# Node numbering, adjacency pieces and the start of layer 0 in a four-layer graph network

## The chip, the core and the metric

One core of a Trainium2 chip runs the whole network in one launch. The metric is the device time of a run in microseconds. The engines named below are PE (TensorE, with PEld for its weight loads), DVE (VectorE), ACT (ScalarE), POOL (GpSimd) and SP (SyncE, which issues most of the DMAs here).

## What is computed

The input `x` has 16 batches of 1024 nodes with 64 features, float32; `adj` is one 1024 x 1024 int32 adjacency for all batches. Four layers follow each other. Each adds its output to its input and normalizes the rows.

```python
x = layernorm(x + L0(x, adj))   # graph attention: leaky_relu(s1[i] + s2[j]), masked softmax, elu
x = layernorm(x + L1(x, adj))   # softplus features, a masked softmax per feature
x = layernorm(x + L2(x, adj))   # like L0, other weights
x = layernorm(x + L3(x, adj))   # 4 heads of masked softmax(h h^T) h, then one outer such layer
```

In layers 0 to 2 the mask is the adjacency; in layer 3 it is `adj + eye > 0`. Entries of `adj` of zero or below count as no edge.

## The kernel before

**Tiles.** P is 128 and C is 8: the nodes are cut into eight chunks of 128, one node to a partition. Node number `p * 8 + c` lies in partition p, chunk c, so a partition holds eight rows of `x` that are neighbours in memory (`load_x`, L641: 2 KB in memory, but eight runs of 256 bytes in the tile `xg`, where four batches share a chunk). The stores at L1549 and L1554 use the same numbering; there both sides are 2 KB runs.

**The adjacency.** `load_adj` (L806) loads eight tiles `adj`, tile c with the rows `p * 8 + c`, each row whole (4 KB), through four buffers. `adjacency` (L813) makes of one tile: `gr`, its 0/1 form in bfloat16 (DVE, L815); on ACT the sum of what lies below zero, kept in `adj_low` (`below`, L817); eight transposes on PE (L821) of every eighth column into PSUM (`paT`); and one copy of that (L822, DVE for even c, ACT for odd c) into `aT`. `aT[:, k, :]` is the mask that chunk k of the neighbours needs for all 1024 nodes, and every one of the eight tiles gives a strip of 128 columns of it. So no mask of layer 0 can start before all eight tiles are done. `adj_low` is checked at the end of the program (L1919): if it is not zero, a general path is run.

**Layer 0 and layer 2** (`gat_layer`, L900). For every pair of batches a chain prepares the factors: `prep_x` transposes x (`pxT`, L919, and its copy `xT`, L920), `prep_s` makes the scores of the nodes (`ps`, L926), `prep_top` reduces them to a largest one (`l_s`, `top`, and an all-reduce on POOL, L937), `prep_p` makes `p` and `q` on ACT, `prep_G` a matmul `pg` (L960) and its exponential `G_l` (L961, one for each half of the nodes, PSUM for one `pg` at a time), and `prep_v` the values `vals_l` (L967). Then, for each batch and chunk k, `unit(k)` makes a mask product `e` on DVE (L980) from G, q and `aT[:, k, :]`, and `product(k, e)` multiplies it on PE with the values: `y_l` (L992) for each chunk and, in layer 0, `u_l` (L1004) for four chunks at once, which adds up the weights.

**What sets the order.** Within `gat_layer`'s loop over batches t and chunks k (L1156), the order on PE, ACT, DVE and POOL is the order in which the code issues the instructions (`manual_schedule`). `behind` (L792) keeps a product back until `lag` more masks are issued: four in layer 0, two in layer 2. `slots` holds the tasks of the chains and of the ends of earlier batches, by (t, k). What comes ahead of the loop, `first(ahead)` (L1663), is ordered by the scheduler: it loads the adjacency, x 2 and 3, the weights and the other x, then makes the eight pieces, one after the other, with one task of the first pair's chain behind each. DMAs of SP are issued in order, and one that needs a buffer back waits for it with all behind it.

**Layer 3.** `aT` gets the diagonal (L1857). Masks multiply `e` on DVE (L1328) ahead of the product on PE (L1335); scores are made on PE (L1320) and exponentiated on ACT (L1324). Scores and masks of a burst of three or five units are issued before the products of the burst before. For the outer layer the adjacency is also needed the other way round, `aN`: `nodes_adj(c)` (L1237) loads the same rows of `adj` again, `convert` turns them into 0/1 (L1242, reading every eighth element) and adds the diagonal. The eight conversions lie in the bursts of the first batch. `aN` is read by the outer layer's sums (L1432).

Of the kernel before, what the change touches and what calls it, by code (L numbers as in the profile page):

```python
# [582 lines left out]
def fast_path(  # L583
# [49 lines left out]
    def xb(b):  # L633
        return xg[b // GB][:, :, b % GB, :]
# [3 lines left out]
        return xg[b // GB][:, c, b % GB : b % GB + 2, :].rearrange("p b d -> p (b d)")  # L638

    def load_x(b):  # L640
        nc.sync.dma_start(xb(b), x[b].rearrange("(p c) d -> p c d", c=C))  # L641


    nc.scalar.preload_act_table_set("natural_log_exp_and_others")
# [159 lines left out]
    adj_v = adj.rearrange("(p c) n -> c p n", c=C)  # L804

    def load_adj(stage):  # L806
        tiles = []
        for c in range(C):
            tiles.append(stage.tile([P, N], I32, tag="adj", name=f"adj{c}", bufs=4))
            nc.sync.dma_start(tiles[c], adj_v[c])  # L810
        return tiles

    def adjacency(stage, a_sb, c):  # L813
        gr = stage.tile([P, N], BF16, tag="gr", name=f"gr{c}")
        nc.vector.tensor_scalar(gr, a_sb, 0.0, None, ALU.is_gt)  # L815
        below = stage.tile([P, N], BF16, tag="below", name="below", bufs=1)
        nc.scalar.activation(below, a_sb, AF.Relu, scale=-1.0, accum_out=adj_low[:, c : c + 1])  # L817
        gr_v = gr.rearrange("p (q k) -> p k q", k=C)
        pt = ps_t.tile([P, C, P], BF16, tag="t", name="paT")
        for k in range(C):  # L820
            nc.tensor.transpose(pt[:, k, :], gr_v[:, k, :], ident16)  # L821
        (nc.scalar.copy if c % 2 else nc.vector.tensor_copy)(aT[:, :, c * P : (c + 1) * P], pt)  # L822

# [7 lines left out]
    def gat_weights(W, a, name, zero_mean, queue):  # L831
        wd = const.tile([P, D], F32, tag=f"{name}_wd", name=f"{name}_wd")
        w1 = const.tile([P, P], F32, tag=f"{name}_w1", name=f"{name}_w1")
        w4 = const.tile([P, 4], F32, tag=f"{name}_w4", name=f"{name}_w4")
        ind = const.tile([P, 2], F32, tag=f"{name}_ind", name=f"{name}_ind")
        s12 = const.tile([P, B // 2, C, 4], F32, tag=f"{name}_s", name=f"{name}_s")
        sums = const.tile([P, B, C], F32, tag=f"{name}_sums", name=f"{name}_sums")
        checks.append((s12, sums))
        a_sb = const.tile([D, 2], F32, tag=f"{name}_a", name=f"{name}_a")
        queue.dma_start(a_sb, a.rearrange("(t o) u -> o (t u)", o=D))  # L840
        for i in range(2):
            queue.dma_start(wd[i * D : (i + 1) * D, :], W)
        return dict(wd=wd, w1=w1, w4=w4, ind=ind, s12=s12, sums=sums, a=a_sb)
# [56 lines left out]
    def gat_layer(w, name, zero_mean, extra, first, own, ordered):  # L900
# [249 lines left out]
        for (t, k), todo in extra.items():  # L1150
            for task in todo:
                at(t, k, task)
        first(ahead)
        if ordered:
            run.enter_context(tc.manual_schedule(engines=in_order))
        for t in range(B + 1):  # L1156
            for k in range(C):
                catch_up()
                if t < B:
                    unit, product, _ = work[t]  # L1160
                    e = unit(k)
                    behind(lambda product=product, k=k, e=e: product(k, e), LAG if zero_mean else 2 * LAG)
                elif t == B and k == 0:
                    drain()
                if t < B or (t == B and k < own):
                    for task in slots.get((t, k), []):
                        task()
# [68 lines left out]

    def nodes_adj(c):  # L1237
        a_sb = l3.tile([P, N], I32, tag="e", name=f"adj3_{c}", bufs=11)
        nc.sync.dma_start(a_sb, adj_v[c])

        def convert():
            nc.vector.tensor_scalar(  # L1242
                aN[:, c, :].rearrange("p (k q) -> p k q", q=P), a_sb.rearrange("p (q k) -> p k q", k=C),
                0.0, None, ALU.is_gt,
            )
# [168 lines left out]
    def head_out(b):  # L1414
# [129 lines left out]
        def rows():  # L1544
            shift = small.tile([P, C], F32, tag="ln_ve", name="ln_shift")
            nc.vector.tensor_tensor(shift, held["less"], held["rstd"], ALU.mult)
            res = ep.tile([P, C, D], F32, tag="m", name="res", bufs=4)
            scaled(res, held["m"], (held["rstd"], shift), range(C))
            nc.sync.dma_start(out[b].rearrange("(p c) d -> p c d", c=C), res)  # L1549

        def finish():
            res = ep.tile([P, C, D], F32, tag="m", name="res", bufs=4)
            nc.vector.tensor_tensor(res, held["m"], bc_last(held["rstd"], D), ALU.mult)
            nc.sync.dma_start(out[b].rearrange("(p c) d -> p c d", c=C), res)  # L1554
# [103 lines left out]
    with tc.tile_pool(name="ps_g", bufs=1, space=bass.MemoryType.PSUM, reuse_waits="tile") as ps_g, tc.tile_pool(  # L1658
        name="ps_u", bufs=2, space=bass.MemoryType.PSUM, reuse_waits="tile"
    ) as ps_u, tc.tile_pool(name="gat0", bufs=2, reuse_waits="tile") as gp:  # L1660
        later = {}

        def first(ahead):  # L1663
            with tc.tile_pool(name="stage", bufs=2, reuse_waits="tile") as stage:
                tiles = load_adj(stage)
                load_x(2)
                load_x(3)
                later["w2"] = gat_weights(L2_W, L2_a, "l2", True, nc.sync)
                later["tasks", "w2"] = gat_setup(later["w2"], "l2", True)
                later["tasks", "w3"] = layer3_weights(gp)  # L1670
                layer1_weights()
                for b in range(4, B):
                    load_x(b)
# [12 lines left out]
        l1["psum"] = lambda name: ps_g.tile([P, 2, HALF], F32, tag="g", name=name).rearrange(  # L1686
            "p i (c q) -> p (i c) q", q=P
        )
        l1_tasks = [prep_l1(0, q) for q in range(2)]
        extra = {}  # L1690
        for t, k in ((2, "w2"), (4, "w3")):
            for i, n in enumerate((2, 3, 4, 5)):
                extra[t, n] = [lambda k=k, i=i: later["tasks", k][i]()]
        for q, todo in enumerate(l1_tasks):
            t = 7 + 2 * q
            places = (t, 0), (t, 2), (t, 4), (t, 6), (t + 2, 2), (t + 2, 7), (t + 3, 5)
            for place, task in zip(places, todo):
                extra.setdefault(place, []).append(task)
        ending = gat_layer(w_0, "l0", False, extra, first, 5, True)
# [278 lines left out]
```

## Time and profile before

| | |
|---|---|
| median of 3 runs | 2076.14 us (2075.71 to 2076.99) |
| the profiled execution | 2073.99 us, its span 2072.2 us |
| PE busy | 1960.6 us, 95% of the span |
| DVE busy | 1795.4 us, 87% |
| ACT busy | 1294.2 us, 62% |
| POOL busy | 69.3 us, 3% |
| mean granted PE clock | 0.978 of full speed |
| DMA | 18.92 MB in 23657 packets |

Spans, durations and waits in the views are of the one profiled execution, counted in microseconds from the start of its span. A row of a timeline gives the start, the time from the first to the last of the instructions in it, the engine, the line, the operation, the tile written and the tiles read, and in brackets how long the engine had been idle and who ended that. A row of a stage gives the busy time of each engine in it with the number of instructions, then the clock that PE was granted (1.00 is full), the mean busy share of the DMA engines and the GB/s that they moved. A row of one line's instructions gives the shortest, median and longest duration in ns. A row of waits gives the total, the number of times and the longest wait in us.

### The profile page before, as it was taken

Reading aid. Unit: us, or ns where it says so; the run is one execution under the profiler, and the core shown is the slowest. Engines: PE = TensorE matmul, PEld = TensorE weight load, DVE = VectorE, ACT = ScalarE, POOL = GpSimd, SP = SyncE. Lnnn points to the kernel's source line nnn. Section 1 sums busy time; section 2 is a strip of 40 time slices with the busy share of each in tenths; the row PEclk is TensorE's granted clock in tenths of the full one; section 3 lists DMA queues with packets and bytes.
Section 4 is the critical chain, followed back from the end, with each engine's and each line's share of the span. In section 5 each row is a group of like instructions: output and inputs, shape, how many; then the busy total and the mean of one; then the engine's idle time right before and its main releaser. Section 6 shows DMA issues by size and latency. Waiting matters only on the chain.

```text
span 2072.2 us, 26628 instructions
## 1 busy us (share of the span) xinstructions
PE 1960.6 (95%) x10041; PEld 851.5 (41%) x10041; DVE 1795.4 (87%) x3147; ACT 1294.2 (62%) x2250; POOL 69.3 (3%) x77
## 2 busy tenths in 40 slices
PE   7999989998888999999999999999999999999985
PEld 4444357843332344343343434334343343433332
DVE  5899988869998777889898898988989889889996
ACT  5456568666778666666666656655665666665543
POOL 0000000000000000000000000000000000000001
PEclk8999999989999999999999999999999999999997
DMA  6000000000000200000000000000000000000000
GB/s 170 1 1 1 1 1 0 1 1 1 1 1 12 70 1 1 1 1 6 1 6 6 1 6 6 1 6 1 6 3 3 6 1 6 6 1 6 1 6 17
DMA packets 23657, 18.92 MB, mean 9 GB/s; under 512 B 19361, under 2 KB 19426, under 8 KB 23522
## 3 DMA queue, kind: packets, MB, share of 16 engines
q1 hardware_dynamic: 23218, 17.11, 2.9%
q8 instruction: 81, 1.33, 0.3%
q14 instruction: 54, 0.44, 0.1%
q10 hardware_dynamic: 304, 0.03, 0.0%
HBM read 12.95 MB, written 4.19 MB: 8 GB/s over the span
## 4 chain that ended last, share of the span: by engine, by line
PE 46%; DVE 38%; ACT 12%; issue 3%; DMA 0%; POOL 0%; SPq 0%; DVEq 0%; POOLq 0%; ACTq 0%
DVE e L1328 13%; PE y L1335 10%; PE s L1320 8%; DVE e L980 6%; PE y_l L992 6%; ACT e L1324 6%; PE po L1712 4%; DVE e L1440 4%; DVE junk L1432 4%; PE u_l L1004 3%; PE y L1447 2%; PE po L1350 2%; ACT e L1427 2%; PE s L1422 2%; DVE v L1360 2%
## 5 line engine op out<-in xcount | busy, mean ns | idle before, releaser
L1324 ACT ACTIVATE e<-s,shift 128x1024 f32<-128x1024 f32 x512 | 542.8, 1119 | 335.2 <-PE s L1320 334.3
L1328 DVE TENSOR_TENSOR e<-e,aT 128x1024 f32<-128x1024 f32 x512 | 600.6, 1217 | 4.9 <-ACT e L1324 4.8
L1335 PE MATMUL y<-e,vals 128*64 128x512 f32 x2048 | 489.5, 600 | 11.0 <-DVE e L1328 5.9
L1320 PE MATMUL s<-hT 64*128 64x512 f32 x2048 | 497.7, 605 | 1.3 <-ACT e L1324 0.9
L980 DVE SCALAR_TENSOR_TENSOR e<-G_l,q,aT 128x1024 f32<-128x1024 f32 x256 | 315.3, 1274 | 10.3 <-ACT G_l L961 10.2
L1320 PEld LDWEIGHTS s<-hT 64*128 64x128 f32 x2048 | 186.9, 187 | 279.6 <-issue 140.3
L992 PE MATMUL y_l<-e,vals_l 128*64 128x512 f32 x1024 | 254.7, 618 | 24.4 <-DVE e L980 22.6
L1335 PEld LDWEIGHTS y<-e,vals 128*64 128x64 f32 x2048 | 134.9, 136 | 277.7 <-issue 189.3
L1440 DVE TENSOR_TENSOR e<-e,aT 128x1024 f32<-128x1024 f32 x128 | 156.3, 1224 | 8.3 <-ACT e L1427 1.9
L1432 DVE SCALAR_TENSOR_TENSOR junk<-e,aN 128x1024 bf16<-128x1024 f32 x120 | 146.1, 1217 | 0.0
L1427 ACT ACTIVATE e<-s,shift 128x1024 f32<-128x1024 f32 x128 | 142.0, 1115 | 1.2 <-PE s L1422 1.1
L1447 PE MATMUL y<-e,h2v 128*64 128x512 f32 x512 | 131.2, 595 | 1.6 <-DVE e L1440 1.6
L1422 PE MATMUL s<-h2T 64*128 64x512 f32 x512 | 131.7, 596 | 0.0
L992 PEld LDWEIGHTS y_l<-e,vals_l 128*64 128x64 f32 x1024 | 62.6, 138 | 159.4 <-issue 75.9
L1712 PE MATMUL po<-hi,aR 128*128 128x512 f32 x256 | 102.4, 401 | 13.6 <-ACT hi L1648 8.6
L1712 PE MATMUL po<-lo,aR 128*128 128x512 f32 x256 | 100.8, 394 | 0.0
L780 ACT ACTIVATE x<-m,bn_shift,bn_rstd 128x64 f32<-128x64 f32 x256 | 88.5, 431 | 2.4 <-DVE bn_shift L771 2.4
L1263 POOL PARTITION_ALL_REDUCE gtop<-top x48 | 42.7, 890 | 1375.8 <-DVE top L1261 1169.0
L1350 PE MATMUL po<-wb,yT 128*128 128x130 f32 x512 | 74.2, 288 | 10.0 <-ACT e L1324 9.4
L1350 PEld LDWEIGHTS po<-wb,yT 128*128 128x128 f32 x512 | 61.9, 190 | 47.4 <-ACT e L1324 45.8
L1422 PEld LDWEIGHTS s<-h2T 64*128 64x128 f32 x512 | 49.8, 188 | 61.2 <-issue 28.4
L1384 ACT COPY zT<-pzT 128x1024 f32<-128x1024 f32 x32 | 32.8, 1025 | 66.9 <-PE pzT L1383 66.9
(241 smaller groups left out, 2028.6 us busy)
## 6 DMA issues: line engine op xcount, KB each, us to landing
adj<-in_adj_dram SPq DMA_DIRECT2D x16, 512.0 KB, 4.2
x<-in_x_dram SPq DMA_DIRECT2D x16, 256.0 KB, 5.0
out_dram<-res SPq DMA_DIRECT2D x16, 256.0 KB, 2.0
wl<-in_L_gnn_Wh_dram SPq DMA_DIRECT2D x2, 64.0 KB, 3.6
wo<-in_L_gnn_Wo_dram SPq DMA_DIRECT2D x1, 64.0 KB, 3.1
l_wd<-in_L_gnn_W_dram ACTq DMA_DIRECT2D x2, 16.0 KB, 4.1
l_wd<-in_L_gnn_W_dram SPq DMA_DIRECT2D x2, 16.0 KB, 2.2
bo<-in_L_gnn_bo_dram SPq DMA_DIRECT2D x1, 32.0 KB, 3.2
```

What stands on the lines that cost most here:

```text
L980: nc.vector.scalar_tensor_tensor(e, G[b - b % 2][:, b % 2, :], pq[b - b % 2][1][:, k, b % 2 : b % 2 + 1], aT[:, k, :], ALU.max, ALU.mult,)
L992: nc.tensor.matmul(held["y"][h * D : (h + 1) * D, :], vals[b][:, k, :], e[:, h * HALF : (h + 1) * HALF], start=(k == 0), stop=(k == C - 1),)
L1320: nc.tensor.matmul(s[:, i, :], hT[rows, k * P : (k + 1) * P], hT[rows, cols], start=True, stop=True)
L1324: nc.scalar.activation(e, s, AF.Exp, bias=shifts[b, n])
L1328: nc.vector.tensor_tensor(e, e, bc_mid(aT[:, k, h * HALF : (h + 1) * HALF], 2), ALU.mult)
L1335: nc.tensor.matmul(held[h][i * D : (i + 1) * D, :], vals[b][:, k, :], e[:, i, :], start=(k == 0), stop=(k == C - 1),)
L1350: nc.tensor.matmul(o[:, j // 2, j % 2, :], held["y"][:, j * P : (j + 1) * P], wb[:, n, :], start=True, stop=True,)
L1422: nc.tensor.matmul(s[:, i, :], hT[rows, (i + k // CH) % 2, k % CH * P : (k % CH + 1) * P], hT[rows, 0, :], start=True, stop=True,)
L1427: nc.scalar.activation(e, s, AF.Exp, bias=shifts[b])
L1432: nc.vector.scalar_tensor_tensor(junk.rearrange("p c q -> p (c q)").bitcast(BF16), e.rearrange("p i q -> p (i q)"), 1.0, aN[:, k, :], ALU. ...
L1440: nc.vector.tensor_tensor(e, e, aT[:, k, :].rearrange("p (i q) -> p i q", i=2), ALU.mult)
L1712: nc.tensor.matmul(po.rearrange("p q k f -> p (q k f)"), aR[:, k, ic * P : (ic + 1) * P], e[:, k].rearrange("p q k f -> p (q k f)"), start ...
```

## The change

Nodes are numbered `c * 128 + p`: chunk c is the 128 rows from `c * 128`. x and the result are read and written in that order. For layer 0 the adjacency is loaded by columns: piece c holds the columns of chunk c for all rows (1024 runs of 512 bytes), into the ring that the masks use, and `aT[:, c, :]` comes from that piece alone. All eight loads are issued without waiting for a buffer, x 2 and 3 between the fourth and the fifth. The sum on ACT of what lies below zero goes; in layer 3, where the rows are loaded again, DVE takes each row's minimum, and the check is that it is not below zero. The conversion there reads and writes in order. Every copy into `aT` is on ACT. Three pieces are made ahead of the loop, behind the third, the fourth and the sixth task of the chain; the other five come in the loop, each behind one of the first five masks of layer 0. While those come, and in the whole first batch, a product waits for one to three masks instead of four.

```diff
     def load_x(b):
-        nc.sync.dma_start(xb(b), x[b].rearrange("(p c) d -> p c d", c=C))
+        nc.sync.dma_start(xb(b), x[b].rearrange("(c p) d -> p c d", c=C))
...
-    def load_adj(stage):
-        tiles = []
-        for c in range(C):
-            tiles.append(stage.tile([P, N], I32, tag="adj", name=f"adj{c}", bufs=4))
-            nc.sync.dma_start(tiles[c], adj_v[c])
-        return tiles
+    def load_adj(c):
+        t = gp.tile([P, C, P], I32, tag="e", name=f"adj{c}", bufs=10)
+        nc.sync.dma_start(t, adj[:, c * P : (c + 1) * P].rearrange("(k p) q -> p k q", p=P))
+        return t
...
-    def adjacency(stage, a_sb, c):
-        gr = stage.tile([P, N], BF16, tag="gr", name=f"gr{c}")
+    def adjacency(a_sb, c):
+        gr = gp.tile([P, C, P], BF16, tag="gr", name=f"gr{c}", bufs=3)
         nc.vector.tensor_scalar(gr, a_sb, 0.0, None, ALU.is_gt)
-        below = stage.tile([P, N], BF16, tag="below", name="below", bufs=1)
-        nc.scalar.activation(below, a_sb, AF.Relu, scale=-1.0, accum_out=adj_low[:, c : c + 1])
-        gr_v = gr.rearrange("p (q k) -> p k q", k=C)
         pt = ps_t.tile([P, C, P], BF16, tag="t", name="paT")
         for k in range(C):
-            nc.tensor.transpose(pt[:, k, :], gr_v[:, k, :], ident16)
-        (nc.scalar.copy if c % 2 else nc.vector.tensor_copy)(aT[:, :, c * P : (c + 1) * P], pt)
+            nc.tensor.transpose(pt[:, k, :], gr[:, k, :], ident16)
+        nc.scalar.copy(aT[:, c, :], pt.rearrange("p k q -> p (k q)"))
...
-        first(ahead)
+        stream = first(ahead) or []
...
-                    behind(lambda product=product, k=k, e=e: product(k, e), LAG if zero_mean else 2 * LAG)
+                    lag = LAG if zero_mean else 2 * LAG
+                    if stream or (t == 0 and not zero_mean):
+                        lag = 1 + k // 3
+                    behind(lambda product=product, k=k, e=e: product(k, e), lag)
+                    if stream:
+                        stream.pop(0)()
...
     def nodes_adj(c):
         a_sb = l3.tile([P, N], I32, tag="e", name=f"adj3_{c}", bufs=11)
-        nc.sync.dma_start(a_sb, adj_v[c])
+        nc.sync.dma_start(a_sb, adj[c * P : (c + 1) * P, :])
...
-            nc.vector.tensor_scalar(
-                aN[:, c, :].rearrange("p (k q) -> p k q", q=P), a_sb.rearrange("p (q k) -> p k q", k=C),
-                0.0, None, ALU.is_gt,
-            )
+            nc.vector.tensor_scalar(aN[:, c, :], a_sb, 0.0, None, ALU.is_gt)
+            nc.vector.tensor_reduce(adj_low[:, c : c + 1], a_sb, AX.X, ALU.min)
...
-            nc.sync.dma_start(out[b].rearrange("(p c) d -> p c d", c=C), res)
+            nc.sync.dma_start(out[b].rearrange("(c p) d -> p c d", c=C), res)
...
         def first(ahead):
-            with tc.tile_pool(name="stage", bufs=2, reuse_waits="tile") as stage:
-                tiles = load_adj(stage)
...
-                for c in range(C):
-                    adjacency(stage, tiles[c], c)
-                    for task in ahead[c : c + 1]:
-                        task()
-                for task in ahead[C:]:
-                    task()
+            tiles = [load_adj(c) for c in range(CH)]
+            load_x(2)
+            load_x(3)
+            tiles += [load_adj(c) for c in range(CH, C)]
...
+            for i, task in enumerate(ahead):
+                task()
+                if i in (2, 3, 5):
+                    adjacency(tiles[(2, 3, 5).index(i)], (2, 3, 5).index(i))
...
+            return [lambda c=c: adjacency(tiles[c], c) for c in range(3, C)]
...
-    check(adj_low, ALU.is_le, 0.0)
+    check(adj_low, ALU.is_ge, 0.0)
```

More of the change, by code (lines that the diff above doesn't have):

```diff
@@ L803, in fast_path @@
     adj_low = const.tile([P, C], F32, tag="adj_low", name="adj_low")
-    adj_v = adj.rearrange("(p c) n -> c p n", c=C)
-    def load_adj(stage):
-        tiles = []
-        for c in range(C):
-            tiles.append(stage.tile([P, N], I32, tag="adj", name=f"adj{c}", bufs=4))
-            nc.sync.dma_start(tiles[c], adj_v[c])
-        return tiles
-    def adjacency(stage, a_sb, c):
-        gr = stage.tile([P, N], BF16, tag="gr", name=f"gr{c}")
+    def load_adj(c):
[4 more added lines that the diff above has]
+        gr = gp.tile([P, C, P], BF16, tag="gr", name=f"gr{c}", bufs=3)
         nc.vector.tensor_scalar(gr, a_sb, 0.0, None, ALU.is_gt)
-        below = stage.tile([P, N], BF16, tag="below", name="below", bufs=1)
-        nc.scalar.activation(below, a_sb, AF.Relu, scale=-1.0, accum_out=adj_low[:, c : c + 1])
-        gr_v = gr.rearrange("p (q k) -> p k q", k=C)
         pt = ps_t.tile([P, C, P], BF16, tag="t", name="paT")
         for k in range(C):
-            nc.tensor.transpose(pt[:, k, :], gr_v[:, k, :], ident16)
-        (nc.scalar.copy if c % 2 else nc.vector.tensor_copy)(aT[:, :, c * P : (c + 1) * P], pt)
+            nc.tensor.transpose(pt[:, k, :], gr[:, k, :], ident16)
+        nc.scalar.copy(aT[:, c, :], pt.rearrange("p k q -> p (k q)"))
     checks = []
@@ L1553, in finish @@
             nc.vector.tensor_tensor(res, held["m"], bc_last(held["rstd"], D), ALU.mult)
-            nc.sync.dma_start(out[b].rearrange("(p c) d -> p c d", c=C), res)
+            nc.sync.dma_start(out[b].rearrange("(c p) d -> p c d", c=C), res)
         units = [
@@ L1663, in first @@
         def first(ahead):
-            with tc.tile_pool(name="stage", bufs=2, reuse_waits="tile") as stage:
-                tiles = load_adj(stage)
[L1666 to L1673, printed above, removed]
-                for c in range(C):
-                    adjacency(stage, tiles[c], c)
-                    for task in ahead[c : c + 1]:
-                        task()
-                for task in ahead[C:]:
-                    task()
+            tiles = [load_adj(c) for c in range(CH)]
+            load_x(2)
+            load_x(3)
+            tiles += [load_adj(c) for c in range(CH, C)]
+            later["w2"] = gat_weights(L2_W, L2_a, "l2", True, nc.sync)
+            later["tasks", "w2"] = gat_setup(later["w2"], "l2", True)
+            later["tasks", "w3"] = layer3_weights(gp)
+            layer1_weights()
+            for b in range(4, B):
+                load_x(b)
+            for i, task in enumerate(ahead):
+                task()
+                if i in (2, 3, 5):
+                    adjacency(tiles[(2, 3, 5).index(i)], (2, 3, 5).index(i))
             l1["pool"] = l1_pools.enter_context(
```

## The prediction, made before the changed kernel ran

> **What bounds the kernel now.** I read the page's list of groups first (PE is busy 1960.6 of 2072.2 us), then the timeline of the first 75 us, then the busy time by stage in steps of 2 us, and last the waits of PE in layer 3 and the timeline of the end. Comparing the two instruction orders, engine by engine, I find that they differ in three places only: before about 50 us, in eight added vector instructions of layer 3, and in the shape of the DMAs. So the sum has three terms.
>
> The timeline of the start, at the steps that count:
>
> ```profile
> 15.12 0.69 DVE L822 COPY aT<-paT 128x1024 bf16<-128x1024 bf16 x1 [2.10 <-PE paT L821]
> ...
> 21.95 1.07 PE L821 MATMUL paT<-ident,gr 128*128 128x128 bf16 x8 [0.25 <-DVE gr L815]
> ...
> 24.09 1.10 ACT L961 ACTIVATE G_l<-pg,up 128x1024 f32<-128x1024 f32 x1
> ...
> 27.42 1.97 PE L919 MATMUL pxT<-ident,x 128*128 128x128 f32 x8
> ...
> 28.68 2.48 DVE L980 SCALAR_TENSOR_TENSOR e<-G_l,q,aT 128x1024 f32<-128x1024 f32 x2 [2.06 <-ACT G_l L961]
> ...
> 31.18 3.58 PE L926 MATMUL ps<-l_w,xT_l 128*128 128x4 f32 x16 [1.79 <-ACT xT_l L920]
> ...
> 34.68 5.03 PE L992 MATMUL y_l<-e,vals_l 128*64 128x512 f32 x16
> ...
> 50.08 1.94 PE L992 MATMUL y_l<-e,vals_l 128*64 128x512 f32 x8
> ```
>
> All eight pieces are transposed before the first mask (28.68). That mask waits for G, not for the adjacency. From 31.18 PE never rests: batch 2's `ps`, batch 0's products from 34.68, batch 1's from 50.08. A mask that comes early therefore gains only what PE can use. The stages (columns: PE, PEld, DVE, ACT, POOL, clock, DMA, GB/s):
>
> ```profile
> 4.00:6.00 2.00, 0.00 (x0) 0.00 (x0) 0.00 (x0) 0.00 (x0) 0.00 (x0) 1.00 1.04 235
> ...
> 8.00:10.00 2.00, 1.10 (x8) 1.08 (x9) 1.86 (x11) 1.47 (x4) 0.00 (x0) 1.00 1.03 422
> ...
> 14.00:16.00 2.00, 2.00 (x20) 1.63 (x19) 0.88 (x2) 1.97 (x4) 0.00 (x0) 1.00 0.72 256
> ...
> 32.00:34.00 2.00, 2.00 (x11) 2.00 (x11) 0.00 (x0) 0.00 (x0) 0.00 (x0) 0.50 1.18 212
> ...
> 38.00:40.00 2.00, 2.00 (x12) 0.44 (x12) 2.00 (x3) 2.00 (x9) 0.00 (x0) 1.00 1.35 222
> ```
>
> The clock is at half from 17 to 37.5 us, so the small `ps` products cost 3.58 us there against 1.90 at 14.91. DMA moves about 235 GB/s in 256-byte pieces (x) and 422 GB/s in 4 KB rows (adjacency).
>
> **Term 1, the start: about +3.2 us.** I walk the new order with durations from these rows.
>
> *DMA.* A piece is 512 KB in 512-byte runs, 1024 of them. Bounds: 512 KB at 422 GB/s is 1.25 us, at 235 is 2.2; I take 1.8, nearer to x's small pieces. The first landed at 7.15; now 7.6, then 9.4, 11.2, 13; after x2 and x3, the last at about 23. The first mask comes later than most of these, so this costs nothing up to about 3 us a piece. Beyond that every mask waits.
>
> *Up to G.* PE no longer puts a transposed piece between x's: `pxT` 10.1 to 12.1 (8 for 1.97), `ps` and one `pg` to 15.4. DVE makes top by 15.8, and the all-reduce returns 2 us later (top at 35.02, down at 37.77 now). PE does pieces 0 to 2 to 18.4. ACT loses eight `below` (1.06 and 0.19 each, 10 us) but copies every aT: its order has three copies (1.01) before p, so p starts at 19.5, G at 20.0 (24.09 now), `vals` (2.0) at 21.1, the second G at 23.4 (its `pg` is done at 23.2), the first mask at 24.5: 4.2 us early. DVE is spared four aT copies of 0.69.
>
> *After it.* DVE's order is e0, gr3, e1, gr4: 1.21 and 0.69 each. gr3 is done at 26.4, and only then can PE transpose piece 3: it has rested from 18.4 to 21.2 and from 23.2 to 26.5, 6 us, in which the old order did this work. A mask's product is a quarter of sixteen records (3.58 at 42.63 in the chain), so 0.9 at full and 1.76 at half speed. From 26.5 PE's queue runs without a gap: piece 3 1.04, `pxT` of batch 2 2.2, `ps` 3.58 (33.3); y0 1.76, piece 4 1.04, y1 1.76 (37.9, clock full again); pieces 5 and 6 1.41 (0.70 each, the row at 14.37), y2 0.9, piece 7 0.8, y3 0.9, u 1.85, y4 0.9, `pg` 1.06, y5 to y7 2.7, u 1.85, `pg` 1.06, `pxT` 1.03. Batch 1's product starts at 52.4, against 50.08: **+2.3**. Queued behind each gr on DVE are the next mask and, behind gr4, batch 2's l_s; who waits is PE. From there the order is the old one and PE is the bound, so the difference stays.
>
> *The clock.* The trace's full speed at 14 to 17 us follows a stretch in which PE streamed without a pause (10.2 to 13.6). The new order has 128x4 products in it, which nearest rows (30 to 34 us, half speed) do not speed up. Without that stretch the second half of `ps`, two pieces and `pg` are slow, G is at 22.6 and batch 1 at 54.9: +4.8 against this trace. The old order without it would lose 1.9 in the same walk, leaving +2.9. Bounds +0.5 (fast before `ps` of batch 2 by luck of phase, whose 3.58 would be 1.9) and +4.8; I take 3.2.
>
> The Trainium skill ("TensorE: Matmul & The Clock Gate", section "Part 1: The HAM clock gate") says some 3.4 us of sustained PE work give the full clock. The trace disagrees for narrow work: at 32 to 34 us PE is 2.00 of 2.00 busy at 0.50. By the rule alone PE, busy from 26.5, would be fast at 30 to 33 and this term about +1.
>
> **Term 2, layer 3: about +1.0 us.** Each of eight conversions loses its stride and gains a reduction to one minimum.
>
> ```profile
> L1242 DVE TENSOR_SCALAR aN<-adj x8: 1082/1084/1094, 673.7 to 731.8; 128x1024 bf16<-128x1024 int32 x8
> ```
> ```profile
> L815 DVE TENSOR_SCALAR gr<-adj x8: 681/693/694, 7.2 to 23.7; 128x1024 bf16<-128x1024 int32 x8
> ```
> ```profile
> 2051.55 0.81 DVE L1914 TENSOR_REDUCE flags<-ok 128x1 f32<-128x640 f32 x1
> ```
>
> Conversion 1.08 becomes 0.69; a reduction of 1024 is 0.81 x 1024/640 less its fixed part (512 take 0.68), 1.21. That is +0.82 each, 6.5 us of DVE. What hides it is PE, which waits for no mask there:
>
> ```profile
> PE y L1335 <- ACT yT L1341: 1.0, 1, 1.0
> PE s L1320 <- ACT e L1324: 0.9, 1, 0.9
> PE po L1350 <- ACT e L1324: 0.6, 1, 0.6
> ```
>
> DVE idles 12.8 us for PE between 677 and 737 (3.35, 2.92, 1.48, 2.01, 3.02). Of these only 1.48 follows the two conversions at 698 and 703, which add 1.64, so there a little gets through. Bounds 0 and 6.5; I take one conversion and a little, 1.0. A gain is excluded: aN is read first past 760 us. The `below` work that this replaces was in term 1.
>
> **Term 3, the end: about +0.8 us.** The last store now has 1024 pieces of 256 bytes where it had 128 of 2 KB.
>
> ```profile
> 2066.78 0.33 SPq L1554 DMA_DIRECT2D out_dram<-res  x1
> ```
>
> Nothing lies beside it. The issue of x's like-shaped load takes 0.55 at least (+0.2); 256 KB at 235 GB/s is 1.1 us, at 422 is 0.6 (+0.5). Bounds: +0.2, if stores pipeline, and +1.8 (x's loads take 3.5 to land, stores 2.0, and the issue); I take 0.8. The earlier 15 stores have cover. The Trainium skill ("DMA: Bandwidth & Descriptors", "Specifications") names 512 bytes as the least for line rate, with read-modify-write below; no run here shows it for stores. By it this term would lean to its upper bound, and adjacency pieces would take 1.25 us.
>
> **Sum.** +3.2 +1.0 +0.8 = +5.0. The profiled execution took 2073.99 (span 2072.2 and 1.8 around it), so 2079.0 for one like it. The runs' median is 2076.14, 2.15 above it, so **2081.1**.
>
> **Rivals.**
> *A, PE pays (forecast), 0.58:* five transposes move from PE's idle time into its full queue. For it: 34.68 onward is gapless. 2080.3 to 2085.
> *B, it evens out, 0.28:* PE gets the full clock early in its new queue (term 1 +0.5 to 2), layer 3 hides all, the store costs 0.3: +1 to +4, 2077 to 2080. Same mechanism, small.
> *C, faster, 0.06:* the mask's 4.2 us lead reaches PE. It needs y0 right behind e0 at 26, which decides from the point where PE runs `pxT` and `ps` of batch 2 inside the rests at 18.4 and 23.2 and the clock is full by 26. Then at best -4.2 to -5, nothing lost later: 2071.5. Against it: `ps` stands ahead of y0 on PE.
> *D, the pieces land slowly, 0.08:* over 3 us for 512-byte runs at a 4 KB pitch. At 4 us each the last lands near 40, gr5 to gr7 hold the masks, batch 1 starts at about 62: +14 with the other terms, 2088 to 2092. For it: nothing here shows such a load.
>
> The measurement can tell about 0.2% (4.2 us) from no change. Slower is A and D, 0.66; same is B, 0.28; faster is C, 0.06. The range leaves out C, the low edge of B and the worst of D: 2077 to 2086.5; the slower cases' own range is 2080.3 to 2087.
>
> **What would show it.** Right: first mask at 24 to 27 us; PE rests of 2 to 4 us on both sides of the second `pg`; first y_l at 33 to 36 after `ps`; batch 1's y_l at 52 to 55; the reductions at 1.2 us with PE waiting under 2 us for masks in 670 to 745; the last store landing 0.5 to 1.5 us later. Wrong: y_l within 3 us of the first mask (C); gr waiting for a DMA after 15 us (D); a half-speed clock ending before 33 us (B).

## The result, and the profile after

| | before | after |
|---|---|---|
| median of 22 runs each, taken together | 2074.28 us (2071.43 to 2076.99) | 2079.01 us (2076.35 to 2082.81) |
| ratio | | 1.0025 [1.0019, 1.0031] |
| the profiled execution, its span | 2073.99, 2072.2 us | 2082.49, 2080.7 us |

The changed kernel is slower by 4.7 us between the medians, or 3.9 to 6.4 us by the interval. The forecast was 2081.1 us, a difference of +5.0 us to the median of three runs known then; that of 22 old runs lies 1.9 us lower. In the experiments below, one run of e7 took 3997.19 us, far from every other, and is left out. The profiled execution of the changed kernel happens to be one of its longest, so its span overstates the difference (+8.5 us); I split that first.

Matched instruction by instruction, the difference between the two profiles is +5.59 us when batch 1's first `y_l` begins and stays at that value to the end of layer 0. It is about 7.9 us after a stretch of half-speed clock at 338 to 342 us that the old kernel's profile doesn't have, 7.5 us through layer 3, 8.9 us at the last `res`, and 8.5 us at the end. Where such stretches fall differs from profile to profile (further down), so I don't count the part after layer 0 as the change's.

The busy times of the page after say which engine pays:

```profile
PE 1966.3 (95%) x10041; PEld 853.5 (41%) x10041; DVE 1797.7 (86%) x3151; ACT 1289.4 (62%) x2238; POOL 69.7 (3%) x77
```

PE has as many instructions as before (10041), but is busy 5.7 us longer (1960.6 before): the same work, more of it at half clock. A part of the 5.7 us is the stretch at 338 us. (The mean granted clock, 0.983 in this profile and 0.978 before, can't show it, since it counts the first 41.3 us as full; see below.) ACT is only 4.8 us less busy, although 10 us of `below` are gone: four more `aT` copies of about 1 us went to it. The timeline of the start (start, time, engine, line, operation, tile written and read, and in brackets the idle time of the engine and who ended it):

```profile
12.35 1.87 PE L921 MATMUL ps<-l_w,xT_l 128*128 128x4 f32 x8
...
14.15 2.07 PE L955 MATMUL pg<-xT_l,l_w 64*128 64x512 f32 x2
16.16 1.87 PE L921 MATMUL ps<-l_w,xT_l 128*128 128x4 f32 x8
...
19.68 2.07 PE L955 MATMUL pg<-xT_l,l_w 64*128 64x512 f32 x2
21.68 1.04 PE L816 MATMUL paT<-ident,gr 128*128 128x128 bf16 x8
...
23.67 0.31 ACT L943 ACTIVATE p<-l_s,down 128x16 f32<-128x16 f32 x1
...
24.07 1.10 ACT L956 ACTIVATE G_l<-pg,up 128x1024 f32<-128x1024 f32 x1
...
25.23 2.08 PE L955 MATMUL pg<-xT_l,l_w 64*128 64x512 f32 x4 [2.51 <-ACT G_l L956]
...
28.50 1.28 DVE L975 SCALAR_TENSOR_TENSOR e<-G_l,q,aT 128x1024 f32<-128x1024 f32 x1 [9.28 <-ACT G_l L956]
...
30.45 1.04 PE L816 MATMUL paT<-ident,gr 128*128 128x128 bf16 x8 [3.14 <-DVE gr L813]
...
33.49 3.42 PE L921 MATMUL ps<-l_w,xT_l 128*128 128x4 f32 x16
36.84 1.98 PE L987 MATMUL y_l<-e,vals_l 128*64 128x512 f32 x4
...
55.67 1.94 PE L987 MATMUL y_l<-e,vals_l 128*64 128x512 f32 x8
```

and of the old kernel:

```profile
24.41 1.07 PE L821 MATMUL paT<-ident,gr 128*128 128x128 bf16 x8 [1.39 <-DVE gr L815]
...
25.41 2.08 PE L960 MATMUL pg<-xT_l,l_w 64*128 64x512 f32 x4
```

The `pg` of the first half of the nodes stands in two rows here, 64 matrix rows for each batch of the pair (14.15 and 19.68, the first and the second `pg` below); the third row (25.23) is that of the second half, both batches side by side.

Three things are to be seen. First, G starts at 24.07, where it started before (24.09): nothing that ACT was spared has arrived. p, which stands ahead of G on ACT, has its `up` and `down` at 19.2, but ahead of it in ACT's order stands the copy of piece 2, whose transposes stand on PE behind the second `pg` and end at 22.7. Second, PE rests 2.51 us ahead of the next `pg` (25.23) and 3.14 us ahead of piece 3 (30.45): together 5.65, against 1.39 and 1.79 in the old kernel. Third, from the third `pg` to batch 1's `y_l` it is now 30.44 us (25.23 to 55.67), and was 24.67 (25.41 to 50.08). In it PE makes five pieces, 3.76 us, and rests 1.6 us more; these are 5.4 of the 5.8 us. The interval also holds more half clock (25.23 to 41.3, and 25.41 to 37.5 before), so a part of these prices is the clock's; e3 and e4 below take that apart.

The clock is at half throughout: 16 `ps` products take 3.42 us at 33.49, and full speed comes only at 41.3 us (37.5 before, after a stretch of full speed at 14 to 17 that is not here). One stage of 2 us (PE, PEld, DVE, ACT, POOL, clock, DMA, GB/s):

```profile
34.00:36.00 2.00, 2.00 (x11) 2.00 (x11) 0.00 (x0) 0.32 (x1) 0.00 (x0) 1.00 1.36 217
```

The column prints 1.00 there although the products take twice their time: it does so in every stage ahead of the first change of clock that a trace records. At the start the clock is to be read from durations.

The adjacency, by the rows of its eight loads (issue in ns, then the landing):

```profile
L808 SPq DMA_DIRECT2D adj<-in_adj_dram x8: 926/1410/2656, 1.8 to 15.5; - x8
...
DMA to landing us min/median/max: 5.7/7.1/8.0
```

The last is issued at 15.5 and is there by 24, ahead of the first mask; no gr waits for a transfer after 12 us. In the stages with the most traffic (6 to 12 and 16 to 20 us) the core moved 283 to 313 GB/s, and 422 in the old kernel's 4 KB rows.

Layer 3, the rows of the conversion and of the new reduction, and PE's waits from 655 to 770 us (total, times, longest):

```profile
L1244 DVE TENSOR_REDUCE adj_low<-adj x8: 1206/1210/1212, 681.9 to 740.5; 128x1 f32<-128x1024 int32 x8
...
L1243 DVE TENSOR_SCALAR aN<-adj x8: 681/684/686, 681.3 to 739.9; 128x1024 bf16<-128x1024 int32 x8
```
```profile
PE y L1334 <- ACT yT L1340: 1.0, 1, 1.0
PE s L1319 <- ACT e L1323: 0.9, 1, 0.9
...
PE po L1349 <- ACT e L1323: 0.6, 1, 0.6
```

Both durations are as estimated, and these three waits of PE are those of before to the tenth. A fourth, 1.2 us against 0.3, is at 665.6 us, ahead of the reductions; no wait for a mask is among layer 3's. Eleven masks behind the reductions, between 708 and 739 us, come 0.6 us later than the others (a difference of 8.13 to the old kernel against 7.53), and from 745 us the difference is 7.54 again. The stores at the end, first of the old, then of the new kernel:

```profile
L1554 SPq DMA_DIRECT2D out_dram<-res x15: 332/332/352, 949.2 to 2066.8; - x15
...
DMA to landing us min/median/max: 2.0/2.0/3.2
```
```profile
L1553 SPq DMA_DIRECT2D out_dram<-res x15: 372/373/399, 956.7 to 2075.7; - x15
...
DMA to landing us min/median/max: 2.5/2.6/2.8
```

A store in pieces of 256 bytes takes 0.6 us more to land (2.6 against 2.0) and 0.04 us more to issue. But the longest landing, 3.2 us in the old kernel, is that of its last store, and the last one of the new kernel takes 2.8: from the start of the last `res` to the end of the span it is 5.76 us, and was 6.15.

### The profile page after: what moved, and what is told of

Read it like the earlier page. It is cut to its first block, busy times and chain, and to the rows that moved or that the text cites. A ratio compares the mean times of both kernels' runs of the same rounds, so it can differ in the third digit from the quotient of the medians.

```text
span 2080.7 us, 26605 instructions
## 1 busy us (share of the span) xinstructions
PE 1966.3 (95%) x10041; PEld 853.5 (41%) x10041; DVE 1797.7 (86%) x3151; ACT 1289.4 (62%) x2238; POOL 69.7 (3%) x77
## 4 chain that ended last, share of the span: by engine, by line
PE 46%; DVE 38%; ACT 12%; issue 3%; DMA 0%; POOL 0%; SPq 0%; DVEq 0%; POOLq 0%; ACTq 0%
DVE e L1327 13%; PE y L1334 10%; PE s L1319 8%; DVE e L975 6%; PE y_l L987 6%; ACT e L1323 6%; PE po L1710 4%; DVE e L1439 4%; DVE junk L1431 3%; PE u_l L999 3%; PE y L1446 3%; PE po L1349 2%; PE s L1421 2%; ACT e L1426 2%; DVE v L1359 2%
## 5 line engine op out<-in xcount | busy, mean ns | idle before, releaser
L987 PE MATMUL y_l<-e,vals_l 128*64 128x512 f32 x1024 | 255.2, 616 | 24.5 <-DVE e L975 22.6
```

What stands on the lines that cost most here:

```text
L987: nc.tensor.matmul(held["y"][h * D : (h + 1) * D, :], vals[b][:, k, :], e[:, h * HALF : (h + 1) * HALF], start=(k == 0), stop=(k == C - 1),)
```

## The experiments

Each edit is one to the changed kernel. All ratios are to the old kernel, run beside it on the same chip. As the forecast is a sum of a start, a reduction and a store, the first four runs take the terms apart; the next four ask what in the start costs the time; the last ask whether the first mask can be had earlier, and whether anything beats the old kernel.

| run | batch 1's `y_l` begins, us | ratio to the old kernel |
|---|---|---|
| old kernel | 50.08 | 1 |
| changed kernel | 55.67 | 1.0025 [1.0019, 1.0031] |
| e1_all_ahead | 50.42 | 1.0003 [0.9994, 1.0012] |
| e2_row_tiles | 50.20 | 0.9995 [0.9986, 1.0004] |
| e3_no_minimum | 54.38 | 1.0025 [1.0014, 1.0036] |
| e4_row_stores | 53.65 | 1.0023 [1.0014, 1.0033] |
| e5_pe_filled | 52.17 | 1.0011 [1.0003, 1.0020] |
| e6_later_chain | 54.33 | 1.0012 [1.0003, 1.0020] |
| e7_ahead_later_chain | 49.94 | 1.0000 [0.9991, 1.0008] |
| e8_old_lag | 57.45 | 1.0035 [1.0023, 1.0048] |
| e9_two_ahead | 55.27 | 1.0017 [1.0008, 1.0026] |
| e10_rows_later_chain | 52.32 | 0.9988 [0.9977, 0.9998] |
| e10_again, the same kernel | 51.61 | 0.9997 [0.9988, 1.0006] |
| e2_again, the kernel of e2 | 50.08 | 0.9993 [0.9982, 1.0005] |

Two cautions. The column of `y_l` is from one profile each. The origin of a span floats against the first load's landing by over 1 us (the third `pg` begins at 24.16 in e5 and 25.51 in e3, with the same order ahead of it), and between batch 1 and the last `res` the profiles add from -2.7 (e10) to +3.3 us (the changed kernel) to it. This goes in part with the half clock recorded there (53 us of it behind batch 1 in e6 and e10, 72 in the changed kernel's profile, but 71 in the old one's too). And one ratio's interval is 2 us to either side.

**All eight pieces ahead of the loop, as columns.**

```diff
             for i, task in enumerate(ahead):
+                if i < C:
+                    adjacency(tiles[i], i)
                 task()
-                if i in (2, 3, 5):
-                    adjacency(tiles[(2, 3, 5).index(i)], (2, 3, 5).index(i))
...
-            return [lambda c=c: adjacency(tiles[c], c) for c in range(3, C)]
...
-                    if stream or (t == 0 and not zero_mean):
+                    if stream:
                         lag = 1 + k // 3
```

> The changed kernel, but all eight pieces are made ahead of the loop, one for each task of the first chain, and layer 0's first batch keeps the old distance of four masks. Theory A (the five late pieces cost the start, since they move from PE's rests into its full queue): batch 1's first y_l comes at 52 to 53.5 us instead of 55.7, and the time falls by 2 to 3.5 us against the changed kernel. Rival R1 (the cost is the column pieces themselves, 512-byte runs and the longer DMA issues): batch 1 stays at 55 to 56 and the time within 1 us of the changed kernel. Rival R2 (the start's difference is only the phase of PE's clock): batch 1 falls by as much as the half-speed stretch ends earlier, and is the same where it ends at the same time.

Measured: 2075.62 us, ratio 1.0003. Its timeline:

```profile
23.12 2.08 PE L955 MATMUL pg<-xT_l,l_w 64*128 64x512 f32 x4 [1.66 <-ACT G_l L956]
...
50.42 1.94 PE L987 MATMUL y_l<-e,vals_l 128*64 128x512 f32 x8
```

The 3.14 us rest is gone (1.66 and 1.36 remain), the stretch of full clock at 14 to 17 us is back, and batch 1 starts where it did in the old kernel. Numbering, column loads, reductions and stores of the change are all still in this kernel; together they cost nothing that can be measured (the interval ends at 2.5 us). So the loss comes with the five late pieces, or with the shorter lag that this edit undoes too; e8 shows that it isn't the lag. Batch 1 came earlier than the 52 to 53.5 us of theory A. Rival R2, the clock, isn't out by this run, since full speed comes at 38.1 us here and at 41.3 in the changed kernel; e3 and e4 settle it. The first mask comes at 26.43, 2.3 us before the old kernel's, and batch 1 none the earlier. (Three pieces stand behind the third `pg` here, so the 27.30 us from it to batch 1 don't compare with the 24.67.)

**Whole row tiles, all ahead, in the new numbering.** Tiles of 4 KB rows again, made in e1's order, eight strips copied by DVE and ACT in turn, without the ACT sum.

```diff
-        nc.sync.dma_start(t, adj[:, c * P : (c + 1) * P].rearrange("(k p) q -> p k q", p=P))
+        nc.sync.dma_start(t, adj[c * P : (c + 1) * P, :])
...
-        nc.scalar.copy(aT[:, c, :], pt.rearrange("p k q -> p (k q)"))
+        (nc.scalar.copy if c % 2 else nc.vector.tensor_copy)(aT[:, :, c * P : (c + 1) * P], pt)
```

> Nodes numbered by rows of 128 as in the changed kernel, and no sum on ACT, but layer 0's tiles are whole rows of 4 KB again, each giving a strip of 128 columns of every chunk's mask, all eight made ahead of the loop, copies shared by DVE and ACT as before. Theory A: G comes 2 to 4 us earlier than before the change, as ACT is free of 10 us, but the first mask waits for the last strip at about 29; batch 1 at 50 to 52.5, the time 0 to 3 us above the old kernel and 2.5 to 5 below the changed one. Rival R1 (it is the numbering, by x's and the results' 256-byte pieces in memory): the time stays within 1 us of the changed kernel.

Measured: 2074.57 us, ratio 0.9995; a second time, beside e10, 2074.05 us and 0.9993 [0.9982, 1.0005]. Whether the pieces are columns or rows makes no difference that can be told.

> Whole row tiles, all pieces ahead, without the later chain, beside it on the same chip. If the later chain is what gains, this is 1 to 2 us slower than the other; if both do the same work in PE's full queue, they differ by less than 1 us.

It was 0.75 us slower than e10_again (2074.05 and 2073.30 us), under the 1 us that would have spoken for the later chain.

**No reduction in layer 3.**

```diff
+    nc.vector.memset(adj_low, 0.0)
...
-            nc.vector.tensor_reduce(adj_low[:, c : c + 1], a_sb, AX.X, ALU.min)
```

> The changed kernel without the eight reductions to a row's minimum in layer 3 (adj_low is set to zero; the check on negative entries is left out). The prediction's second term gave the eight reductions, net of the faster conversions, 1.0 us. By the trace of the changed kernel, which is as late at 750 us as at 670, it is nothing: the time stays within 0.5 us of the changed kernel, and in the trace masks up to 740 come 0.6 us earlier and those past 750 do not. By the prediction's term: 1 us or more faster than the changed kernel.

Measured: 2078.76 us, ratio 1.0025, as the changed kernel. The interval alone would leave room for 1 us; the trace of the changed kernel, where the difference after the eight reductions is what it was before them, does not. In the trace of this run the eleven masks between 708 and 739 come 1.0 us earlier against the others, and those past 745 do not.

```profile
33.77 1.98 PE L923 MATMUL ps<-l_w,xT_l 128*128 128x4 f32 x16
...
54.38 1.94 PE L989 MATMUL y_l<-e,vals_l 128*64 128x512 f32 x8
```

**Stores in rows of 2 KB.**

```diff
-            nc.sync.dma_start(out[b].rearrange("(c p) d -> p c d", c=C), res)
+            nc.sync.dma_start(out[b].rearrange("(p c) d -> p c d", c=C), res)
```

> The changed kernel with the old form of the stores, 128 pieces of 2 KB (rows of the result come out in the old order of nodes, so it is permuted). The prediction's third term gave the 256-byte pieces 0.8 us at the end. By that term the time from the last multiplication (res) to the end of the span falls by 0.5 to 1.5 us. By the trace of the changed kernel, in which that stretch is 5.1 us against 5.5 before, it changes by under 0.5 us.

Measured: 2079.41 us, ratio 1.0023, with 5.84 us from the last `res` to the end (5.76 with 256-byte pieces). The store costs nothing. This profile shows something else: here full clock came at 33.4 us (34.05 in e3), with an order of the start that is the same.

```profile
33.01 2.02 PE L921 MATMUL ps<-l_w,xT_l 128*128 128x4 f32 x16
...
39.45 0.62 PE L816 MATMUL paT<-ident,gr 128*128 128x128 bf16 x8 [1.29 <-DVE gr L813]
...
53.65 1.94 PE L987 MATMUL y_l<-e,vals_l 128*64 128x512 f32 x8
```

`ps` takes 2.02 instead of 3.42, and still batch 1 is 3.57 us later than in the old kernel. With a fast PE the pieces are late on DVE: l_s of batch 2 and the masks stand ahead of each gr, and PE waits 1.29 and 0.43 us for it. In e3 too batch 1 is 4.3 us late. Counted from the third `pg`, both take 28.9 us, 4.2 more than the old kernel, though their full clock comes 3.5 to 4.1 us before its 37.5: it isn't the clock alone. Half clock or full, the late pieces cost about 3.6 to 5.6 us.

**PE kept busy in its second rest**, with products that nobody reads.

```diff
+                        if k == 0:
+                            pt = ps_a.tile([P, HALF], F32, tag="acc", name="fill")
+                            for _ in range(3):
+                                nc.tensor.matmul(
+                                    pt[:, :256], ident, vals[0].rearrange("p c d -> p (c d)")[:, :256],
+                                    start=True, stop=True,
+                                )
                         stream.pop(0)()
```

> The changed kernel with three 128x256 products without a reader on PE, between the second pg and piece 3, where PE rests for 3.1 us (27.3 to 30.4 in the changed kernel's trace). They take the rest and nothing else, so only PE's clock can gain. Theory A with the clock as a part of it: a stretch of PE work without a pause is longer by 3 us, full speed comes at 31 to 34 us in every run instead of 33 to 41, batch 1's first y_l comes at 52.8 to 53.7 and the time falls by 0.5 to 2 us against the changed kernel, to a ratio of 1.0015 to 1.002 against the old one. Rival R2 (the whole start is the clock): batch 1 at 50 to 51 and no difference from the old kernel. Rival R3 (clock without weight): as the changed kernel within 0.5 us.

Measured: 2076.93 us, ratio 1.0011.

```profile
29.38 0.62 PE L816 MATMUL paT<-ident,gr 128*128 128x128 bf16 x8 [0.61 <-DVE gr L813]
...
31.59 1.94 PE L921 MATMUL ps<-l_w,xT_l 128*128 128x4 f32 x16
```

Piece 3 now takes 0.62 us and `ps` 1.94: full clock from 28.3, and batch 1 at 52.17, both earlier than theory A had them. From the third `pg` to batch 1 it is 28.01 us, against 30.44 in the changed kernel and 28.90 in e4. So 1 to 2.5 us of the loss is clock that the rest costs; the remainder, over 3 us against the old kernel's 24.67, is the pieces and the waits for gr.

**The second pair's chain later**, so that y0 comes ahead of `ps` on PE (near to what rival C needs).

```diff
+            if b == 2 and not zero_mean:
+                places = (-2, 3), (-2, 3), (-2, 4), (-2, 4), (-2, 5), (-2, 7), (-1, 1), (-1, 3), (-1, 4), (0, 4)
```

> The changed kernel with the preparation of the second pair of batches (pxT, ps, its top) moved from behind the first mask to behind the fourth to sixth, and what follows from it by one to two masks. The prediction's rival C needed y_l right behind the first mask. Theory A (PE's whole queue up to batch 1 counts, whatever its order): first y_l at 30 to 32 us instead of 36.8, but batch 1 only at 52 to 54.5; the time 0.5 to 2.5 us below the changed kernel, through the clock, which wide products release earlier than narrow ones. Rival R4 (what costs is that masks and products stand behind batch 2's ps in the order): batch 1 at 49 to 50.5, the time at the old kernel's or below.

Measured: 2077.92 us, ratio 1.0012.

```profile
31.34 1.98 PE L987 MATMUL y_l<-e,vals_l 128*64 128x512 f32 x4
...
54.33 1.94 PE L987 MATMUL y_l<-e,vals_l 128*64 128x512 f32 x8
```

Batch 0's first product starts 5.5 us earlier, batch 1's only 1.3 us. An early product is worth little, since `ps` comes into the same full queue behind it. Full clock came at 36.35, not at 41.3. The ratio is better than that start explains; in this profile 2.5 us were won after batch 1, and I can't say that they belong to the edit.

**Both edits, all ahead and the later chain.**

> Column pieces, all eight ahead of the loop (as e1_all_ahead), and the second pair's preparation moved as in e6_later_chain. Theory A: the transposes lie in PE's rests again, products start earlier, and the clock is full earlier: first y_l at 31.5 to 34, batch 1 at 49 to 50.5, the time 0 to 2 us below the old kernel. If the order of the second pair is without weight: as e1_all_ahead, within 0.5 us.

Measured: 2075.29 us, ratio 1.0000.

```profile
31.43 0.62 PE L816 MATMUL paT<-ident,gr 128*128 128x128 bf16 x8 [1.37 <-DVE gr L813]
...
49.94 1.94 PE L987 MATMUL y_l<-e,vals_l 128*64 128x512 f32 x8
```

It isn't better than e1 by anything that can be told. But beside e6 it shows the late pieces once more: the chain is the same, neither profile has the full clock at 14 to 17 us, and with the pieces ahead and the old lag batch 1 begins at 49.94 instead of 54.33. A part of that is the clock, full from 30.4 here and from 36.35 in e6.

**The old lag of four with the late pieces.**

```diff
-                    if stream or (t == 0 and not zero_mean):
-                        lag = 1 + k // 3
```

> The changed kernel, but in layer 0's first batch a product waits for four masks again, as before the change. Theory A: PE's rests grow, as products stand behind more masks and transposes: first y_l at 40 to 42 us, batch 1 1.5 to 2 us later than in the changed kernel (55 to 57.5), and the time 1 to 2.5 us above it. Without weight of the order of products: within 0.5 us of the changed kernel.

Measured: 2082.57 us, ratio 1.0035.

```profile
38.76 1.03 PE L816 MATMUL paT<-ident,gr 128*128 128x128 bf16 x8 [1.47 <-DVE gr L813]
...
57.45 1.94 PE L987 MATMUL y_l<-e,vals_l 128*64 128x512 f32 x8
```

y0 starts at 41.80, PE rests 1.47 and 1.04 us more for pieces whose masks' products are held back, and from the third `pg` to batch 1 it is 32.72 us, 2.3 more than with the short lag. The ratios' intervals overlap; the trace has the change's short lag worth about 2 us. So the lag hides a part of the loss and is not its cause.

**Two pieces ahead, six late.** It takes piece 2's copy away from in front of p.

```diff
-                if i in (2, 3, 5):
-                    adjacency(tiles[(2, 3, 5).index(i)], (2, 3, 5).index(i))
+                if i in (2, 3):
+                    adjacency(tiles[i - 2], i - 2)
...
-            return [lambda c=c: adjacency(tiles[c], c) for c in range(3, C)]
+            return [lambda c=c: adjacency(tiles[c], c) for c in range(2, C)]
```

> Only pieces 0 and 1 are made ahead of the loop, pieces 2 to 7 behind the first six masks. In the changed kernel `up` is there at 19.2 us, but p starts at 23.7, because the copy of piece 2 stands ahead of p on ACT and its transposes (21.7 to 22.7) stand behind the second pg matmul on PE. Here p has only two copies ahead of it. Theory 'the third piece holds p': G_l starts at about 21.8 (24.1 in the changed kernel), the first mask at 26.2, batch 1's products begin 1.3 to 1.7 us earlier than in the changed kernel (2.3 less one more piece, 0.6 to 1.0, in PE's full queue), ratio to the old kernel about 1.0017. Rival 'PE's queue alone sets it': the first mask is earlier but six pieces now stand in the full queue, batch 1's products begin at the same time or up to 1 us later, ratio 1.0025 to 1.003.

Measured: 2079.49 us (old kernel 2075.53 beside it), ratio 1.0017.

```profile
25.81 1.28 DVE L975 SCALAR_TENSOR_TENSOR e<-G_l,q,aT 128x1024 f32<-128x1024 f32 x1 [7.01 <-ACT G_l L956]
...
55.27 1.94 PE L987 MATMUL y_l<-e,vals_l 128*64 128x512 f32 x8
```

It was piece 2 that held G: G starts at 21.37 and the first mask is 2.7 us earlier. But batch 1 gains only 0.4 us of that, less than the 1.3 to 1.7 expected: a sixth piece stands in the full queue, and PE waits 0.71 and 0.69 us for gr. By the trace the rival is nearer; the ratio is the theory's, and its interval (to 1.0026) just reaches the rival's 1.0025.

**Row tiles, all ahead, and the later chain.** e2 with e6's edit.

> Candidate for a version better than both: whole row tiles of the adjacency, all eight made ahead of the loop, lag of four, and the second pair's chain three slots later, so that batch 0's products come ahead of ps on PE. Theory 'PE's full queue sets it': PE has the same work from the first mask on, so batch 1's products begin at 49.5 to 50.2 and the ratio to the old kernel is 0.999 to 1.000. Rival 'an early product helps': batch 0's products start at 31 to 33 and the lead is kept, ratio 0.998 to 0.999.

Measured: 2073.95 us, ratio 0.9988; its batch 1 begins at 52.32 in the profile, later than either theory said. So I ran it again.

> The kernel of the whole row tiles with the later chain once more, because its first interval (0.9977 to 0.9998) lies at the edge of what the measurement can tell. If it is really faster than the old kernel by 1 to 4 us, the ratio is again under 1.000 with its interval mostly below; if the first ratio came from the clock's phase, 0.9995 to 1.0005.

Measured: 2073.30 us, ratio 0.9997 [0.9988, 1.0006], beside e2's 0.9993. The first interval was not repeated. No version here beats the old kernel by an amount that this measurement can tell.

## Why the prediction held, by its steps

**The verdict and its cause held.** The forecast was that five transposes move from PE's idle time into its full queue, and that PE pays (rival A). The changed kernel against e1, with e8 against the lag and e3 and e4 against the clock, shows that the late pieces cost the time, and the third `pg` to batch 1 shows PE paying it. That the sum came so close, +5.0 against +4.7, is partly luck: term 1 was too small and the other two were too big. Of the signs named in advance, the rests, the reductions and the waits of layer 3 came as said. The first mask (28.50, not 24 to 27), the first y_l (36.84, not 33 to 36) and batch 1 (55.67, not 52 to 55) came later, and the last store did not land later than before.

**Term 1, forecast +3.2, bounds +0.5 to +4.8; measured +5.6 in the changed kernel's profile, +4.3 and +3.6 in e3's and e4's (4.2 in both if counted from the third `pg`).** The rests were right (2.8 and 3.3 us forecast, 2.51 and 3.14 measured), and so, within 1 us, were the loads. What failed is the step "Up to G":

- *The first mask was forecast at 24.5 and came at 28.50.* I let the first part run at full clock by the old trace and put the lack of it into a bound. The clock did not rise there, in this profile or in any other with this order, and each half of `ps` took 1.87.
- *`pg` was under-counted.* Its two matmuls, parted by `ps` and pieces, take 2.07 us each at half clock; side by side the pair takes 2.08. The walk has one `pg`, with `ps`, up to 15.4, and no second one before the pieces.
- *Piece 2 was taken as done ahead of p.* It came 4 us later, behind the second `pg`, and ACT's order made p and G wait for its copy. Little of the late mask reaches batch 1: in e9 it is 2.7 us earlier, and batch 1, with one more piece in PE's queue, 0.4.
- *The lower bound was wrong.* I took an early full clock to save all but 0.5 us. In e4 it came at 33.4 and +3.6 remained, in part since DVE then delivers gr too late (PE waits 1.72 us for it). Queued on DVE behind l_s and the masks, gr has a cost that I had named, and put at nothing.

The clock part went as its row said rather than by the rule: PE was 2.00 of 2.00 busy at 34 to 36 with `ps` at half speed. The Trainium skill ("TensorE: Matmul & The Clock Gate", section "Part 1: The HAM clock gate"), by which some 3.4 us of sustained work give the full clock, would have put full speed at about 34 here (an estimate, from PE's start at 30.45); it came at 41.3. In e3 and e4 the same order had it at 34.05 and 33.37, 3.3 and 3.4 us behind that start, as the figure gives. So the same order goes either way from run to run, and neither reading is a safe forecast for one run.

**Term 2, forecast +1.0; measured 0.** The prices were right (1210 and 684 ns). What I let "get through" at the third idle stretch was eleven masks late by 0.6 us, which PE's own work covered.

**Term 3, forecast +0.8; measured 0** (-0.4 us by the tails of the old and the changed kernel's profiles, -0.1 between the changed kernel's pieces and e4's rows). A typical store does land 0.6 us later, which was the estimate. But the step took 2.0 us, the landing of the other stores, for the last one as well; that one takes 2.8 to 3.2 in either form.

**The rivals.** B's small sum did not come: e3 and e4 had its condition, a full clock at 33 to 34, and its price was wrong. Only with PE kept busy in its rest (e5, full clock from 28.3) did the start come near it, at +2.1. C's order was tried in e6 (y0 ahead of `ps`, though at 31.34 and not at 26), and its gain stayed away: PE's queue behind y0 is full. D is out: 512-byte runs landed as walked. At 283 to 313 GB/s a piece of 512 KB takes some 1.7 to 1.9 us (an estimate), near the 1.8 walked with and above the 1.25 of line rate.

## What to carry to other kernels

When work is moved later to let a first result out earlier, look at the queue into which it goes, not at the result: an engine that rests before a point and never after it loses what is moved across. Read in each engine's order what stands ahead of the first consumer; here a copy that nobody needed yet held p. A reduction or a smaller transfer beside other work may well be free, and shows so when the difference between two traces is the same before and behind it.

## What was not expected of the hardware

- Two 64-row matmuls `pg` next to each other take as long as one by itself (2.08 and 2.07 us at half clock). Parting them costs 2 us.
- The early stretch of full clock, at 14 to 17 us, is in the profiles of the old kernel, e1 and e2, which put `paT` transposes between those of x, and in none of the changed kernel, e3, e4, e5, e6, e8 and e9, which don't. e7 and e10, which do, lack it too, so those transposes are not enough by themselves. The kernel of e10 has it in its second profile (e10_again) and e2's in both: the same program goes one way or the other from run to run. The first row is e10's, the second e10_again's:

```profile
17.15 3.52 PE L915 MATMUL ps<-l_w,xT_l 128*128 128x4 f32 x16
```
```profile
14.69 1.90 PE L915 MATMUL ps<-l_w,xT_l 128*128 128x4 f32 x16
```

- A rest of PE of 1.81 us in layer 1 (337.25 is its end in the changed kernel's profile) is in all 14 profiles. In two of them, the changed kernel's and e10_again's, 3.41 us of half speed follow 1 us behind it (granted 0.57 over 338 to 342), in the others none; what decides stays open. Every stretch between two changes of the clock in these traces lasts a multiple of 3.41 us.
- One kernel's runs lie 6 us apart. In the changed kernel's 22 runs this goes with the mean granted clock: the eight at 0.983 took 2078.44 to 2082.81 us, the ten at 0.985 2076.35 to 2079.50. In the old kernel's runs beside the experiments no such relation shows, so its scatter stays unexplained. Spans of single profiles can't be compared to better than about 3 us.
